# The second attention of a two-layer graph network in a fixed order on three engines, with its routing in seven steps, paced weight loads and later index copies

## The chip, the cores and the metric

The kernel runs on one core of a Trainium2 chip. A core has five engines, each with its own queue of instructions that it takes in order: TensorE (PE in the profile; its weight loads are shown apart as PEld), VectorE (DVE), ScalarE (ACT), GpSimd (POOL), and SyncE (SP), which here only starts DMAs. An engine waits for another, or for a DMA, at a semaphore. The metric is the device time of one execution in microseconds (us); the median of several runs counts.

## The reference

The input is x (2708 rows of 256) and a sparse 0/1 matrix adj (2708 x 2708). All arithmetic is in float32. Two layers, each an attention over the graph and then a mixture of eight experts:

```
x = x + elu(softmax(where(adj > 0, q k^T / 16, -9e15)) v)         # q, k, v from layernorm(x)
x = x + top2_experts_0(layernorm(x))                               # hidden 1024, own layernorm, weights sum to 1
h = layernorm(x) @ W_fc + b_fc
s = (h @ w_att[:256])[:, None] + (h @ w_att[256:])[None, :] + b_att
x = x + softmax(where(adj > 0, s, -1e9), axis=1) @ h               # "the second attention"
x = x + top2_experts_1(layernorm(x))                               # hidden 512, weights = softmax probabilities
```

In the second attention the score of row i and key j is a term of i plus a term of j. The term of i falls out of the softmax, so the numerator is a product of the 0/1 mask with rows `exp(s_j) * h_j`, and the denominator the same product with `exp(s_j)`.

## The kernel before

**Tiles.** The 2708 rows are 22 tiles (NT) of 128, the last of 20. The stages follow one another: first attention, first experts, second attention, second experts, final sum.

**Second attention** (`layer1_attention`, L602 on). The query tiles are taken in groups, `GROUPS = [6, 6, 4, 3, 3]`; this text calls them G0 to G4. Each group runs over all 22 key tiles k. `attend` (L700) multiplies, for each query tile of the group, the mask of key tile k with the two halves (`parts`) of that key's value row, one matmul each (L708), into an accumulator in PSUM; the short last key tile comes at the end (L714). The masks lie in SBUF as fp8 (`mTs`, one per block of 512 queries) and ScalarE turns the piece that a key needs into float32 (`key_masks`, L681), two keys ahead; `m` has six buffers.

G0 is special: `keys_and_values` (L739) also makes the keys' values, one tile per turn of its loop. VectorE takes statistics of the row (`norm_begin`, L209 to L211), GpSimd raises the variance to the power -1/2 (L215), VectorE normalises (`norm_end`, L219), TensorE transposes (L225), ScalarE copies, TensorE multiplies with W_fc (L640), ScalarE applies the exponential (L646 to L648), GpSimd copies the result into `parts` (L653) and adds the bias to the kept row (L654), and VectorE computes the rest that the first part has lost (`second_part`, L660). `PAUSE` dummy matmuls (L747) stand at the start of G0.

**Routing.** When a group is done, `evict` (L731) copies its accumulators out and puts a generator `finish` for each tile into `line`. `line.step()` (L281), called once per key (in G3 and G4 once per two keys), starts a waiting tile every `line.gap` steps and takes each running tile to its next `yield`. For one tile the steps are: `over_sum`; the new row and its statistics (with the power on GpSimd); in `Experts.route` (L916) the normalised row (L219), two index copies on GpSimd (L940) and the second copy of the row (L944); the gate's logits, top two and `sel` (L961 to L982); the exponential on ScalarE (L984); two small matmuls that count the rows before this one (L987, L988), then at once on VectorE the weights, the target rows `to` (L989 to L1002), and two indirect scatters by GpSimd (L1005) into the DRAM buffer `disp`. Row buffers come in six pairs. The tiles of one group are so routed during the next ones.

**Second experts.** Rows are gathered by expert in chunks of 128, called slots. Each slot reads its rows from `disp` (`xg`, by SP, L1168) and its expert's weights (1154 KB) into one of four ring buffers (`ring`, by an indirect DMA of GpSimd, L1153; a slot whose expert is in the buffer already skips the transfer). `open` (L1126), called at the start of G2, makes the ring and guesses the first four experts; `fill` (L1145) loads these by plain DMAs on SP. `begin` (L1118) is called when 14 tiles are routed and a few keys have passed; it runs `place` (L1020), a row of small VectorE operations on the counts that makes the tables `token_row` and `weight_row` for the first 20 slots, and fetches the first three slots' rows and weights. A second call of `place` inside the slots makes the tables of the rest.

**Order.** SP runs in program order throughout. The second experts' slots run in program order on TensorE, ScalarE and VectorE. In the second attention only G0 is in program order (on these three and GpSimd); in G1 to G4 a scheduler orders each engine's instructions by its own estimates. Several of the lines named here are those of helpers.

Of the kernel before, what the change touches and what calls it, by code (L numbers as in the profile page):

```python
# [20 lines left out]
P = 128  # L21
N = 2708
D = 256
# [29 lines left out]
PAUSE = 12  # L53
# [16 lines left out]
def adj_ffn_kernel(ctx: ExitStack, tc: tile.TileContext, a: dict, out: bass.AP):  # L70
# [147 lines left out]
    def normed(dst, src, mean, factor):  # L218
        nc.vector.tensor_scalar(dst, src, mean, factor, op0=ALU.subtract, op1=ALU.mult)  # L219
# [80 lines left out]
    def layer0_attention(line):  # L300
        with ExitStack() as scope, ExitStack() as until_last:
# [237 lines left out]
            for b, (b0, nb, ts_) in enumerate(BLOCKS):  # L539
# [6 lines left out]
                for k in range(NT):  # L546
# [38 lines left out]
                    if b == last and k == LAG + 2:  # L585
                        experts0.open()
                        experts0.begin()
# [14 lines left out]
    def layer1_attention(mTs, kept, line, first_masks):  # L602
        with ExitStack() as scope:
# [32 lines left out]
            def values(t, xT):  # L636
                r = P
                ps = misc.tile([P, GROUP, P], F32, name="misc").rearrange("p g n -> p (g n)")
                for c in range(DC):
                    nc.tensor.matmul(  # L640
                        ps[:r, : VALUES + 1 + E], xT[:, c, :r], wfc[:, c, :],
                        start=(c == 0), stop=(c == DC - 1),
                    )
                e = e_tail if t == NT - 1 else pool.tile([P, VALUES + 1], F32, name="e", bufs=3)
                q, weight = ROWS[t], e[:r, VALUES : VALUES + 1]
                nc.scalar.activation(weight, ps[:r, VALUES : VALUES + 1], AF.Exp)  # L646
                nc.scalar.activation(e[:r, :VALUES], ps[:r, :VALUES], AF.Copy, scale=weight)
                nc.scalar.activation(  # L648
                    logits[:q, t], ps[:q, VALUES + 1 : VALUES + 1 + E], AF.Copy,
                    scale=spread_of[:q, t : t + 1],  # L650
                )
                if t < NT - 1:
                    nc.gpsimd.tensor_copy(parts[:r, t, 0, : VALUES + 1], e[:r])  # L653
                nc.gpsimd.tensor_add(kept[:q, t], kept[:q, t], bfc_b[:q])  # L654
                return e

# [8 lines left out]
            tails = {}  # L665
# [8 lines left out]
            def key_masks(ts_, k):  # L674

                masks = {}
                for b in sorted({t // GROUP for t in ts_}):
# [3 lines left out]
                    nc.scalar.copy(m[:, : q1 - q0], mTs[b][:, k, q0 - b * BN : q1 - b * BN])  # L681
                    masks.update({t: m[:, t * P - q0 : t * P - q0 + ROWS[t]] for t in here})
# [56 lines left out]
            def keys_and_values(ts_, accs):  # L739
# [5 lines left out]
                idle = misc.tile([P, GROUP, P], F32, name="misc").rearrange("p g n -> p (g n)")  # L745
                for _ in range(PAUSE):
                    nc.tensor.matmul(  # L747
                        idle, ident, wfc.rearrange("p c n -> p (c n)")[:, : GROUP * P],
                        start=True, stop=True,
                    )  # L750
                next(masks_of_keys)
                stats, xn, xT, e = {}, {}, {}, {}
                for i in range(-3, NT + LAG1 - 1):
                    if 0 <= i - 1 < NT - 1:
                        second_part(i - 1, e.pop(i - 1))
                    if i + 3 < NT:
                        stats[i + 3] = norm_begin(i + 3)
                    if 0 <= i + 2 < NT:
                        xn[i + 2] = norm_end(i + 2, *stats.pop(i + 2))
                    if 0 <= i + 1 < NT:  # L760
                        xT[i + 1] = columns(i + 1, xn.pop(i + 1))
                    if 0 <= i < NT:
                        e[i] = values(i, xT[i])
# [7 lines left out]
            g0, total, since = 0, None, 0  # L771
            for g, wide in enumerate(GROUPS):
                if g == 2:
# [6 lines left out]
                    guess = experts1.open([i * (n // RING) * E // (n + GROUP) for i in range(RING)])  # L780
# [5 lines left out]
                if g == 0:  # L786
                    with tc.manual_schedule(engines={
                        mybir.EngineType.PE, mybir.EngineType.Activation,
                        mybir.EngineType.DVE, mybir.EngineType.Pool,
                    }):  # L790
                        keys_and_values(ts_, accs)
                for k in range(NT if g else 0):
# [6 lines left out]
                    if g > 0 and not experts1.begun and experts1.routed >= experts1.early:  # L799
                        since += 1  # L800
                        if since > 2:
                            experts1.begin()
# [8 lines left out]
                g0 += wide  # L811

# [38 lines left out]
    class Experts:  # L851
# [64 lines left out]
        def route(self, t, x, logits=None):  # L916
# [19 lines left out]
            else:  # L936
                xt = rows2[0][:r, :D]
                normed(xt, x[:r], mean, once)
            for j in range(2):
                nc.gpsimd.tensor_copy(  # L940
                    rows2[j].bitcast(I32)[:r, D : D + 1],
                    token[:r, 0 if own_norm else j, t : t + 1],
                )
            (nc.vector if own_norm or self.begun else nc.gpsimd).tensor_copy(  # L944
# [43 lines left out]
            nc.tensor.matmul(ps[:, :E], ones, seen, start=False, stop=True)  # L988
            nc.vector.reciprocal(den[:r, 1:2], den[:r, 0:1])  # L989
# [30 lines left out]
        def place(self, s0, s1):  # L1020
# [8 lines left out]
            if all_chunks:  # L1029
# [3 lines left out]
                self.pads = [partial(self.pad, end, e) for e in range(E)]  # L1033
            tab = one.tile([P, NT, E], F32, name="tab")
# [21 lines left out]
            nc.vector.tensor_sub(change, offset[:, 1:], offset[:, : E - 1])  # L1056
            n = s1 - s0
# [5 lines left out]
            nc.vector.tensor_reduce(self.expert[:, s0:s1], passed, AX.X, ALU.add)  # L1063
            row = one.tile([P, n], F32, name=f"row{s0}")
# [23 lines left out]
            else:  # L1088
# [5 lines left out]
                nc.vector.tensor_sub(self.taken, last, first)  # L1094

# [22 lines left out]
        def begin(self):  # L1118
# [3 lines left out]
            self.place(0, FULL_AFTER[self.early])  # L1122
# [3 lines left out]
        def open(self, likely=None):  # L1126
# [12 lines left out]
            if likely:  # L1139
# [3 lines left out]
                return self.fill(likely)  # L1143

        def fill(self, likely):  # L1145

            for i, e in enumerate(likely):
                nc.sync.dma_start(self.ring[i], self.packed_weights[0][e * P : (e + 1) * P, :])
                yield
# [43 lines left out]
        def slots(self, two, ps_mm, ps_tp, ps_acc, line):  # L1193
# [76 lines left out]
            def slot(s, s1):  # L1270
# [18 lines left out]
                if not placed and (not line.busy() or s + AHEAD == n):  # L1289

                    line.finish()
                    self.place(n, SLOTS)
# [125 lines left out]
```

## Time and profile before

| | |
|---|---|
| median of 3 runs | 1299.15 us (1295.99 to 1305.99) |
| the profiled execution, its time | 1312.22 us |
| its span in the profile | 1310.4 us |
| mean granted TensorE clock | 0.968 |
| busy: TensorE, its weight loads, VectorE, ScalarE, GpSimd | 1209.5, 964.8, 543.6, 438.4, 424.3 us |
| first attention, first experts | 0 to 528.9, to 863.9 us |
| second attention, keys and values with G0 | 872.0 to 947.9 us |
| G1, G2, G3, G4 | to 986.6, 1025.3, 1047.9, 1076.1 us |
| second experts | to about 1280 us |
| final sum | to 1310.4 us |

The stage edges are read from the first matmul of each. A row of the profile names line, engine and operation, what it writes and reads, and its shape. "Idle before" is the time that the engine stood still before an instruction, with what ended the wait; the releaser is inferred from semaphores. The granted clock is the share of full speed at which TensorE was let run. Only waits on the engine that sets a stage's end cost time.

### The profile page before, as it was taken

The page shows a single profiled execution, that of the slowest core. Times are in us where ns is not written, and L with a number is a line of the kernel's source. Part 1 is how long each engine was busy: PE and PEld are TensorE (multiplying, and loading weights), DVE is VectorE, ACT ScalarE, POOL GpSimd, SP SyncE. Part 2 cuts the span into 40 slices and gives each one's busy share as a digit, 9 for nine tenths or more (in the row PEclk, how much of TensorE's full clock was granted, in tenths as well). Part 3 has the DMA queues.
Part 4 walks back from the last instruction along what each step waited for, and adds up shares of the span by engine and source line. Part 5 has one row for each costly group of instructions (what it writes and reads, how often), then busy time and mean ns, then how long its engine had stood idle before and what let it go on. Part 6 is the DMA issues. An engine that isn't in the chain of part 4 may idle for free. (4 is left out here: it accounts for less than half of the span.)

```text
span 1310.4 us, 20893 instructions
## 1 busy us (share of the span) xinstructions
PE 1209.5 (92%) x7098; PEld 964.8 (74%) x7098; DVE 543.6 (41%) x2087; ACT 438.4 (33%) x1282; POOL 424.3 (32%) x553
## 2 busy tenths in 40 slices
PE   7999999999999999999999999989986878999990
PEld 4776666566566665799999999958886767899880
DVE  6613833634626435632121212137764656322114
ACT  3222222112112222532323232326653446544440
POOL 4100111110110203443333433335453556555450
PEclk9999999999999999999999999999998988999995
DMA  8601365997937717274668644540004125544457
GB/s 264 222 1 66 106 177 141 247 239 190 247 90 180 152 57 294 79 214 127 214 214 285 191 133 142 166 106 3 2 30 173 38 69 163 178 138 130 136 178 258
DMA packets 107243, 197.83 MB, mean 151 GB/s; under 512 B 26754, under 2 KB 81719, under 8 KB 100987
## 3 DMA queue, kind: packets, MB, share of 16 engines
q1 hardware_dynamic: 77276, 110.09, 30.2%
q0 software_dynamic: 27040, 83.56, 20.1%
q10 hardware_dynamic: 2814, 2.77, 0.7%
q8 instruction: 59, 0.97, 0.3%
q14 instruction: 54, 0.43, 0.1%
HBM read 263.63 MB, written 66.12 MB: 252 GB/s over the span
## 5 line engine op out<-in xcount | busy, mean ns | idle before, releaser
L1224 PEld LDWEIGHTS mm<-xe,ring 128*128 128x128 f32 x2192 | 266.8, 195 | 28.0 <-issue 14.0
L1224 PE MATMUL mm<-xe,ring 128*128 128x128 f32 x2192 | 276.2, 280 | 12.0 <-ACT xe L1211 5.0
L1240 PE MATMUL acc<-ring,hT 128*128 128x256 f32 x1096 | 266.6, 381 | 3.4 <-ACT hT L1232 3.4
L1232 ACT ACTIVATE hT<-mm,ring 128x128 f32<-128x128 f32 x548 | 156.0, 368 | 255.8 <-issue 196.6
L1240 PEld LDWEIGHTS acc<-ring,hT 128*128 128x128 f32 x1096 | 195.1, 191 | 24.1 <-ACT hT L1232 4.0
L447 PE MATMUL s<-g,xnT 128*128 128x512 f32 x420 | 206.4, 606 | 3.3 <-DVE mT L459 3.3
L504 PE MATMUL acc<-v,p 128*128 128x257 f32 (+1 forms) x880 | 209.1, 389 | 0.0
L1246 DVE TENSOR_TENSOR y<-acc,bias 128x256 f32<-128x256 f32 x92 | 39.0, 424 | 361.2 <-PE acc L1240 353.9
L504 PEld LDWEIGHTS acc<-v,p 128*128 128x128 f32 (+1 forms) x880 | 153.3, 190 | 18.1 <-issue 0.8
L1153 POOL DMA_INDIRECT ring<-L_ffn_packed,weight_row x98 | 103.5, 1057 | 186.4 <-issue 150.1
L708 PE MATMUL acc<-parts,m 128*128 128x266 f32 x924 | 134.6, 301 | 15.4 <-ACT m L681 10.4
L708 PEld LDWEIGHTS acc<-parts,m 128*128 128x128 f32 x924 | 121.9, 192 | 23.6 <-ACT m L681 12.3
L215 POOL TENSOR_TENSOR ln_rs<-ln_rs,minus_half 128x2 f32<-128x2 f32 x88 | 65.6, 746 | 219.2 <-DVE ln_rs L211 201.5
L1005 POOL DMA_INDIRECT disp<-row,to x88 | 87.4, 993 | 141.7 <-issue 49.2
L459 DVE TENSOR_SCALAR mT<-s 128x512 fp8e4<-128x512 f32 x105 | 71.9, 687 | 128.0 <-ACT p L458 126.1
L458 ACT ACTIVATE p<-s 128x512 f32<-128x512 f32 x105 | 62.2, 594 | 164.7 <-PE s L453 163.4
L447 PEld LDWEIGHTS s<-g,xnT 128*128 128x128 f32 x420 | 75.3, 192 | 50.2 <-issue 41.9
L1258 POOL DMA_INDIRECT xd<-y,xg x45 | 71.1, 1579 | 77.8 <-issue 30.5
L453 PEld LDWEIGHTS <-apart 128*128 128x128 fp8e4 x420 | 32.7, 99 | 61.2 <-issue 61.2
L681 ACT CAST m<-mT 128x512 fp32r<-128x512 fp8e4 (+4 forms) x168 | 70.4, 471 | 16.9 <-PE acc L708 10.2
L334 DVE TENSOR_SCALAR apart<-adj 128x677 fp8e4<-128x677 int32 x80 | 40.7, 512 | 59.0 <-DMA adj<-in_adj_dram 58.6
L1251 POOL DMA_INDIRECT xd<-y,xg x47 | 47.1, 1003 | 21.6 <-PE tp L1201 7.9
(226 smaller groups left out, 1153.9 us busy)
## 6 DMA issues: line engine op xcount, KB each, us to landing
adj<-in_adj_dram SPq DMA_DIRECT2D x84, 338.5 KB
L_ffn_packed<-in_L_ffn_W_dram SPq DMA_DIRECT2D x16, 1024.0 KB
xg<-disp SPq DMA_DIRECT2D x98, 129.0 KB
L_ffn_packed<-in_L_ffn_W_dram SPq DMA_DIRECT2D x16, 512.0 KB
neighbours<-mT SPq DMA_DIRECT2D x5, 1408.0 KB
mT<-neighbours SPq DMA_DIRECT2D x5, 1408.0 KB
xin<-in_x_dram SPq DMA_DIRECT2D x42, 128.0 KB
ring<-L_ffn_packed SPq DMA_DIRECT2D x4, 1154.0 KB
```

The lines of the kernel that those rows point to most:

```text
L215: nc.gpsimd.tensor_tensor(rs[:r, 1], rs[:r, 0], minus_half[:r], ALU.pow)
L447: nc.tensor.matmul(ps[:kr, :nb], xnT[:, c, k0 : k0 + kr], g[:, c, :nb], start=(c == 0), stop=False,)
L459: nc.vector.tensor_scalar(mT[:kr, k, :], ps[:kr, :nb], -BIG / 2, None, ALU.is_gt, saturate=False,)
L504: nc.tensor.matmul(accs[j][:r], p[keys, q0 : q0 + r], v[keys, k, :], start=(k == 0), stop=(k == NT - 1),)
L681: nc.scalar.copy(m[:, : q1 - q0], mTs[b][:, k, q0 - b * BN : q1 - b * BN])
L708: nc.tensor.matmul(acc[:r], masks[t], parts[:, k, i], start=(k == 0 and i == 0), stop=False,)
L1005: nc.gpsimd.indirect_dma_start(disp[:], bass.IndirectOffsetOnAxis(ap=to[:r, j : j + 1], axis=0), rows2[j][:r], None,)
L1153: nc.gpsimd.indirect_dma_start(w, None, packed[:], bass.IndirectOffsetOnAxis(ap=self.weight_row[:, s : s + 1], axis=0), bounds_check=E * P ...
L1224: nc.tensor.matmul(ps[:, i, :], w[:, c * hidden + f * P : c * hidden + (f + 1) * P], xe[:, c, :], start=(c == 0), stop=(c == DC - 1),)
L1232: nc.scalar.activation(hT[:, f, :], ps[:, i, :], AF.Gelu, bias=w[:, b1 + f : b1 + f + 1])
L1240: nc.tensor.matmul(ps, hT[:, f, :], w[:, w2 + f * D : w2 + (f + 1) * D], start=(f == 0), stop=(f == hc - 1),)
L1258: start = nc.gpsimd.indirect_dma_start(xd[:], at, y, None, bounds_check=N - 1, oob_is_err=False, compute_op=ALU.add)
```

## The change

1. From G0 on, the whole second attention stands in program order on TensorE, ScalarE and VectorE; GpSimd is in program order in G0 alone, as before.
2. `route` yields once more, between the two counting matmuls and the VectorE operations behind them: seven steps instead of six.
3. `place` yields four times. `begin` returns a generator that is stepped once per key in G3 and G4, from the moment that 14 tiles are routed. In the first experts and at the second call it is run through at once.
4. `fill` puts a one-column ScalarE copy ahead of each ring load. It reads the mask that was converted last and writes the ring buffer, so the load waits for it.
5. In layer 1 the index copies depend on the normalised row, so that they stand behind it.
6. In G0 the statistics of a later tile come ahead of `second_part`, and the bias add is a call of its own, one turn later.
7. The dummy matmuls have half the width (256 columns) and write G0's first accumulator; there are 28 at the start, and three more among the first transposes.

```diff
-PAUSE = 12
+PAUSE = 28
...
-                nc.gpsimd.tensor_add(kept[:q, t], kept[:q, t], bfc_b[:q])
                 return e
+
+            def add_bias(t):
+                r = ROWS[t]
+                nc.gpsimd.tensor_add(kept[:r, t], kept[:r, t], bfc_b[:r])
...
                     nc.scalar.copy(m[:, : q1 - q0], mTs[b][:, k, q0 - b * BN : q1 - b * BN])
+                    converted_last[0] = m
...
-                idle = misc.tile([P, GROUP, P], F32, name="misc").rearrange("p g n -> p (g n)")
-                for _ in range(PAUSE):
-                    nc.tensor.matmul(
-                        idle, ident, wfc.rearrange("p c n -> p (c n)")[:, : GROUP * P],
-                        start=True, stop=True,
-                    )
+                def busy(n):
+                    for _ in range(n):
+                        nc.tensor.matmul(
+                            accs[0][:, :D], ident, wfc[:, 0, :D], start=True, stop=True
+                        )
+
+                busy(PAUSE)
...
                 for i in range(-3, NT + LAG1 - 1):
+                    if i + 3 < NT:
+                        stats[i + 3] = norm_begin(i + 3)
+                    if 0 <= i - 1 < NT:
+                        add_bias(i - 1)
                     if 0 <= i - 1 < NT - 1:
                         second_part(i - 1, e.pop(i - 1))
-                    if i + 3 < NT:
-                        stats[i + 3] = norm_begin(i + 3)
...
                     if 0 <= i + 1 < NT:
                         xT[i + 1] = columns(i + 1, xn.pop(i + 1))
+                        if i < 1:
+                            busy(1 - i)
...
-            g0, total, since = 0, None, 0
+            scope.enter_context(tc.manual_schedule(engines={
+                mybir.EngineType.PE, mybir.EngineType.Activation, mybir.EngineType.DVE,
+            }))
+            g0, total, beginning = 0, None, None
...
-                    guess = experts1.open([i * (n // RING) * E // (n + GROUP) for i in range(RING)])
+                    guess = experts1.open(
+                        [i * (n // RING) * E // (n + GROUP) for i in range(RING)],
+                        lambda: converted_last[0],
+                    )
...
-                        since += 1
-                        if since > 2:
-                            experts1.begin()
+                        beginning = experts1.begin()
+                    if beginning:
+                        next(beginning, None)
...
+                row = normed(xt, x[:r], mean, once)
             for j in range(2):
-                nc.gpsimd.tensor_copy(
+                index = nc.gpsimd.tensor_copy(
                     rows2[j].bitcast(I32)[:r, D : D + 1],
                     token[:r, 0 if own_norm else j, t : t + 1],
                 )
+                if not own_norm:
+                    tc.add_manual_dep(
+                        index.ins, row.ins.name,
...
+                        reason="no sooner than the row",
+                    )
...
             nc.tensor.matmul(ps[:, :E], ones, seen, start=False, stop=True)
+            if not own_norm:
+                yield
...
-            self.place(0, FULL_AFTER[self.early])
+            return self.begin_steps()
+
+        def begin_steps(self):
+            yield from self.place(0, FULL_AFTER[self.early])
             rows_ = [self.fetch_rows(s) for s in range(AHEAD)]
             self.fetched = [(self.fetch_weights(s), rows_[s]) for s in range(AHEAD)]
...
-        def fill(self, likely):
+        def fill(self, likely, pace):
             for i, e in enumerate(likely):
+                nc.scalar.copy(self.ring[i][:, :1], pace()[:, :1])
                 nc.sync.dma_start(self.ring[i], self.packed_weights[0][e * P : (e + 1) * P, :])
                 yield
```

The four new yields of `place` stand behind the counts (with the ends of the regions), behind the chunk offsets, behind the slots' experts, behind `token_row` (with `taken`), and so ahead of `weight_row`.

## The prediction

> **What bounds the kernel.** I read the busy times by stage first, with stage edges set at the first matmul of each stage in the timeline. Columns: stretch; busy us and instructions of each engine; granted TensorE clock; DMA share; GB/s.
>
> ```profile
> core 0: us, PE busy (x) PEld busy (x) DVE busy (x) ACT busy (x) POOL busy (x), PEclk, DMA share, GB/s
> 528.90:863.90 335.00, 332.89 (x2280) 306.25 (x2280) 87.00 (x329) 114.22 (x380) 128.02 (x105) 0.99 0.57 171
> 872.00:947.90 75.90, 68.96 (x407) 57.61 (x406) 54.35 (x163) 48.45 (x146) 40.29 (x74) 0.93 0.12 38
> 947.90:986.60 38.70, 34.57 (x278) 32.89 (x277) 23.50 (x145) 21.65 (x59) 16.59 (x29) 1.00 0.17 58
> 986.60:1025.30 38.70, 24.89 (x184) 23.41 (x184) 20.75 (x131) 11.13 (x33) 17.19 (x35) 0.87 0.30 121
> 1025.30:1047.90 22.60, 19.30 (x142) 17.70 (x138) 13.69 (x87) 10.41 (x31) 13.21 (x21) 0.92 0.12 42
> 1047.90:1076.10 28.20, 21.43 (x145) 16.58 (x142) 16.90 (x104) 11.63 (x48) 15.11 (x21) 0.89 0.25 72
> 1076.10:1142.20 66.10, 56.06 (x343) 50.01 (x344) 30.52 (x143) 38.62 (x100) 38.65 (x44) 0.89 0.54 167
> ```
>
> TensorE is full in the first experts (332.89 of 335.00) and not in the second attention (keys and values from 872.0; groups G1 to G4 from 947.9, 986.6, 1025.3, 1047.9). G2 has two thirds of G1's matmuls and takes the same 38.7 us. So I asked who TensorE waited for between 947.9 and 1076.1 (total us, times, longest):
>
> ```profile
> PE misc L987 <- DVE sel L982: 11.2, 1, 11.2
> PE acc L708 <- ACT m L681: 10.4, 7, 2.0
> PE acc L708 <- issue: 3.3, 2, 1.7
> ```
>
> Then the timeline around the 11.2 us (start, us, engine, line; in brackets the idle time before it and its releaser):
>
> ```profile
> 989.09 0.41 POOL L940 COPY row<-token 128x1 int32<-128x1 int32 x1 [7.01 <-DMA disp<-row,to]
> 997.17 0.18 POOL L940 COPY row<-token 128x1 int32<-128x1 int32 x1 [5.07 <-DMA disp<-row,to]
> 1001.87 0.72 POOL L215 TENSOR_TENSOR ln_rs<-ln_rs,minus_half 128x2 f32<-128x2 f32 x1
> 1002.63 0.41 DVE L219 TENSOR_SCALAR row<-kept,ln_mv,ln_rs 128x256 f32<-128x256 f32 x1 [12.38 <-POOL ln_rs L215]
> 1004.56 0.17 PE L987 MATMUL misc<-sel,before 128*128 128x8 bf16 x1 [11.23 <-DVE sel L982]
> ```
>
> The chain: an index copy (L940) for a later tile stands in GpSimd's queue ahead of the power of this tile (L215), and waits 7.01 and 5.07 us until an earlier scatter has freed its row buffer. VectorE waits for the power, TensorE for VectorE's `sel`. The scatters are late because the four ring loads (1154 KB each) leave together: DMA share 0.99 to 1.02, 383 to 429 GB/s from 984 to 994. Elsewhere the same copy waits about 1.5 us. The 10.4 us on L681 is ScalarE's order: at 966.72 it waited 3.02 us for VectorE's `p` (L984), with four mask copies behind it, and TensorE waited 1.72 us for them.
>
> **The clock.** The same columns, two falls and what came after:
>
> ```profile
> 875.10:878.50 3.40, 0.85 (x4) 0.40 (x4) 3.15 (x14) 0.91 (x4) 2.20 (x3) 1.00 0.77 230
> 882.00:885.40 3.40, 3.08 (x7) 1.74 (x8) 2.40 (x7) 1.21 (x5) 2.10 (x5) 0.50 0.64 193
> 885.40:888.80 3.40, 3.40 (x12) 2.92 (x13) 2.67 (x8) 1.60 (x6) 2.11 (x4) 0.50 0.00 0
> 1021.90:1025.30 3.40, 1.99 (x18) 1.46 (x18) 2.69 (x20) 1.49 (x7) 1.22 (x3) 1.00 0.00 0
> 1025.30:1028.70 3.40, 3.20 (x16) 2.86 (x13) 3.25 (x19) 3.26 (x10) 2.02 (x2) 0.50 0.22 78
> ```
>
> The clock fell to 0.50 after 3.4 us that held 1.99 us of matmuls, and did not rise after 3.4 us that held 3.08. The Trainium skill ("TensorE: Matmul & The Clock Gate", what's actually happening) says half rate follows a window of about 3.4 us that is idle, full rate one that is busy. By that rule the partial bubble at 1021.9 costs no clock; by the row it costs half of 3.4 us. I take the row: every stall of over about 1.4 us is counted with some clock behind it. Where they differ: a new 3.5 us wait (below) would by the rule hardly cost clock (first expert slots gain 4.5), by the row it does (2.5).
>
> **Part by part, against the profiled execution (1312.22 us).**
>
> *Start of keys and values.* Before: nine dummy matmuls (L747, 0.85 us each) run ahead of TensorE's branch, three behind it; the first real transpose starts at 876.64, matmuls run at half clock from 878.5 to 888.8, and the first attend (L708) starts at 886.72. After: 28 dummies of half the width (0.43 us) all stand behind the branch, three more among the first transposes. TensorE finishes real work at 863.94; its branch took 865.4 to 868.8, so I start the dummies at 869. Half clock until the first full busy window ends (875.1) gives 7.1 of them, the other 20.9 take 8.9: done at 884.0. To the first attend, by program order: transposes, three dummies and two value products 3.8 us, then a bubble, since tile 3's normalised row now stands behind tile 0's `second_part`, which waits for the whole value chain; 6.6 us together: 890.6, 3.9 late. Steady part: from 900 on the period is 3.03 us where TensorE needs 2.63; the 0.2 us waits on `xn` (14 times) come from a loop: statistics, power (0.74) on GpSimd, parts copy (0.40) behind it, `second_part` (0.95), next statistics. With statistics ahead of `second_part`, and the bias add (0.72) moved, that loop opens; VectorE needs 2.4 to 2.55 us a tile. Attend 18: 890.6 + 18 x 2.63 = 937.9 against 940.3: **-2.4**. Bounds: +1 (start at 871.8, one window later) to -6 (clock up a window sooner, no bubble). The middle, since both edges have one near row each.
>
> *G1.* 252 matmuls x 0.1286 = 32.4, tail 1.2, six routing pairs 0.6, eviction 0.4: 34.6 against 38.7. Routing in seven steps puts `sel` two steps ahead of its matmul and the exponential one step ahead of the masks that it could hold up. Per tile VectorE's round (back part 0.8, next tile's `lg` to `sel` 0.85, over_sum 0.7, statistics 1.35, power and its latency 1.0, row 0.4) is 5.1 us beside TensorE's 4.7: it slips 0.4 a tile, 2.2 in six tiles, within a slack of 2.5. **-4.0** (-2 to -4.1).
>
> *G2.* 168 x 0.1286 = 21.6, tail 0.7, rest 1.3: 23.6 against 38.7: **-15.1**; that is 11.2, smaller waits of 2.5, and the half clock from 1004.6 to 1008.2 (1.8). The ring loads now each wait for a one-column ScalarE copy that reads a converted mask, four keys apart: 4.6 us for 1154 KB, which takes 2.8 at 410 GB/s. Nearest row for that copy is a 128x128 mask copy, 0.30: four cost 1.2 us of a ScalarE that is busy 11 of 38.7. The index copies now stand behind the row, so GpSimd's power no longer waits for a landing. The scatter itself has no such cover, nor needs it: its next user is six tiles on. A rule against the pacing: "DMA: Bandwidth & Descriptors" (queues, rings) has each DMA engine take turns between rings by packets. If turns were even, a scatter would land in about 3 us instead of 1.5, and pacing would buy nothing. The row says 7.0 and 5.1; I take it. Bounds -11 (only the long wait goes) to -15.6.
>
> *G3.* 16.2 + 0.7 + 0.8 = 17.7 against 22.6: **-4.9** (waits 1.73, 1.36, 0.2; half clock 1.7). Bounds -3 to -5.
>
> *G4.* Matmuls as in G3, 17.3, but here the early tables come in, some 24 VectorE operations (4 us from 1057 to 1061), now spread over five keys. GpSimd's order has the three ring fetches (1.33 each with their gaps) and tile 14's two scatters (2.6) ahead of tile 16's power: from 10.2 us into the group (`weight_row`) to 16.8, so power at 17.5, `sel` at 20, where TensorE wants it at 16.5. A new wait of 3.5 at L987; behind it stand the tail products and all expert slots. The first chunk (`xg`) is not late: `token_row` at 9.0, loads about 4.5 later by the rows at 1061 to 1065, wanted at 20. 17.3 + 0.4 + 3.5 + 0.5 = 21.7 against 28.2: **-6.5** (-3 to -10). Of the old waits here, 5.1 us are ScalarE's on a releaser that the profile calls remote; nothing in the change touches those by name, so I take 4 off: **-2.5**.
>
> *First expert slots.* 9 us of matmuls ran at half clock after that stall, 4.5 lost; with a 3.5 us wait in front, **-2.5** (0 to -4.5). The exponential/Gelu table switches stay. The second table comes one slot later (3.7 us); its rows are wanted at slot 17, nine slots on: nothing. From 1142 to the end (steady 3.73 us a slot, two DMA stalls) nothing changes but the start.
>
> Sum: 2.4 + 4.0 + 15.1 + 4.9 + 2.5 + 2.5 = **31.4**. Profiled execution about 1281. The median of the runs is 1299.15, 13 us below the profiled one, and I don't know in which waits; the same 31.4 gives **1267.7**.
>
> **Rivals.**
> *A, ScalarE and VectorE still hold up TensorE:* fixed order doesn't remove the 10.4 us on L681, as the exponential stays in line ahead of masks; only ring and index pay: 11.2 + 1.8 + 2.4: about 1283.7. For: VectorE's round (5.1) is longer than TensorE's share (4.7). Against: the extra step's slack.
> *B, all of it:* no remote waits, tile 16 not late, clock full in the slots: 31.4 + 4 + 3.5 + 2 + 2 = 43: about 1256.
> *C, slower:* one mechanism: in fixed order VectorE stands at L219 until GpSimd's power, which stands behind two scatters (2.4) that themselves wait for `to`, which now waits for the scatter of four tiles before to land. With both in the round it is 5.1 + 2.4 and whatever of the landing shows; from 6.55 us a tile on (17 tiles x 1.85 = 31.4) the gain is gone; at 7.5 (no landing at all), 17 x 2.8 = 47.6: 1299 + 16 = about 1315. Against: VectorE's own front part (0.85 + 0.7 + 1.35) runs beside the scatters, and four tiles are over 18 us.
> *D, pacing doesn't pace:* ScalarE may convert up to six masks ahead, so loads could follow at 2.5 us, under their 2.8. Then the queues stay full for 11 us, but the power is no longer behind a landing; VectorE might meet late buffers once: 6 us lost: 1274.
>
> **Numbers.** Forecast 0.60, A 0.17, B 0.10, C 0.05, D 0.08. Range 1253 to 1287: it takes in A and most of B, and leaves out C and a worse start. A measurement of this kernel tells about 1% (13 us) from no change. Faster by over 1% (below 1286): 0.60 + 0.10 + 0.08 + 0.14 of A = 0.92; within 1%: 0.03 of A and 0.02 of C; slower 0.03.
>
> **What would show it.** Right: no idle time over 2 us on L987 in G2, G2 under 25 us; ring loads apart, DMA share well under 1 over 10 us; L225 no longer waiting on `xn`, period 2.63; dummies done near 884, clock 0.50 until about 875. A wait of about 3.5 us at the last L987 of G4. Wrong: L681 waits of 1.5 us or more remain (A); L219 waits for GpSimd of over 3 us in every tile (C); first attend later than 892.

## The result and the profile after

The changed kernel takes **1292.06 us** (median of 9 runs, 1288.55 to 1296.54); beside it the kernel before took 1298.27 (9 runs, 1294.61 to 1305.99). The ratio is 0.9946, with a 95% interval from 0.9922 to 0.9969: 6 us off, within the 1% that the forecast called no change. Forecast were 31.4 us off and 1267.7. Measured again on two chips, each time with the kernel before beside it, the change gave 0.9934 (0.9912 to 0.9955) and 0.9892 (0.9852 to 0.9933). On the last of these chips, called the slower one below, the kernel before took 1312.15 us instead of about 1300, so only ratios and traces are compared between chips.

The profiled execution took 1296.54 us, with a span of 1294.8. The stretches that answer to those of before, edges again at the first matmul of each stage (keys and values with G0, G1, G2, G3, G4 with the hand-over, first expert slots):

```profile
core 0: us, PE busy (x) PEld busy (x) DVE busy (x) ACT busy (x) POOL busy (x), PEclk, DMA share, GB/s
872.00:943.70 71.70, 70.47 (x453) 63.77 (x452) 49.62 (x156) 47.26 (x143) 41.20 (x67) 1.00 0.13 40
943.70:980.10 36.40, 34.08 (x279) 32.88 (x277) 28.71 (x151) 20.96 (x57) 18.21 (x34) 1.00 0.09 33
980.10:1007.60 27.50, 22.52 (x185) 21.74 (x185) 17.52 (x96) 13.01 (x36) 14.12 (x29) 1.00 0.61 218
1007.60:1027.80 20.20, 19.01 (x141) 18.02 (x138) 15.06 (x79) 10.40 (x32) 10.79 (x19) 0.92 0.10 35
1027.80:1059.60 31.80, 20.03 (x144) 16.93 (x142) 24.63 (x133) 11.59 (x50) 19.02 (x30) 0.89 0.21 63
1059.60:1124.40 64.80, 54.37 (x343) 48.24 (x344) 33.70 (x159) 38.91 (x101) 38.49 (x48) 0.92 0.52 170
```

G2 is 11 us shorter, G1 and G3 by 2.3 and 2.4; G4 with the hand-over is 3.6 us longer. VectorE is busy there for 24.63 us where it was busy for 16.90. TensorE's waits from 943.7 to 1062 (total us, times, longest):

```profile
PE misc L1012 <- DVE sel L1007: 12.2, 10, 3.5
PE tp L1237 <- issue: 3.4, 1, 3.4
PE misc L1053 <- DVE seen L1023: 2.9, 1, 2.9
PE acc L713 <- ACT m L685: 0.5, 2, 0.3
```

L1012 is L987 of before, L713 is L708, L685 is L681, L1053 is L1026, L1237 is L1201. The one wait of 11.2 us is gone and so are those on ScalarE's masks (10.4 to 0.5). In their place stand ten smaller waits on VectorE's `sel`, 12.2 us in all, and at the end of G4 a wait of 3.4 that the profile puts down to "issue". TensorE's first transpose of the experts (L1237) needs a PSUM buffer that VectorE's eviction (L739) has to free, and VectorE ends that copy at 1059.5, just before the transpose at 1059.61. (The releaser is inferred here from those times; in a later run, below, the profile itself names the eviction.)

In G2 there is a round. VectorE, GpSimd (start us, us, engine, line; idle time before and its releaser in brackets):

```profile
983.95 0.41 DVE L219 TENSOR_SCALAR row<-kept,ln_mv,ln_rs 128x256 f32<-128x256 f32 x1 [1.04 <-POOL ln_rs L215]
987.00 0.17 DVE L1029 TENSOR_REDUCE to<-hot 128x2 int32<-128x16 f32 x1
987.95 1.04 POOL L1032 DMA_INDIRECT disp<-row,to  x1 [2.88 <-issue]
989.29 0.98 POOL L1032 DMA_INDIRECT disp<-row,to  x1 [0.30 <-issue]
990.29 0.74 POOL L215 TENSOR_TENSOR ln_rs<-ln_rs,minus_half 128x2 f32<-128x2 f32 x1
991.07 0.41 DVE L219 TENSOR_SCALAR row<-kept,ln_mv,ln_rs 128x256 f32<-128x256 f32 x1 [2.56 <-POOL ln_rs L215]
```

From one row (L219) VectorE takes 3.2 us to `to`; 0.8 us later GpSimd starts two scatters, 2.3 us; behind them stands the next tile's power, 0.74; and VectorE waits for it. The round is 991.07 - 983.95 = 7.12 us a tile. TensorE has 5.2 us of matmuls in such a round (5.23 from 998.18 to 1005.28) and waits for the rest: 1.22, 1.88 and 1.88 us on `sel` in three rounds. This is the mechanism of rival C, at a milder size, and no landing is in it.

In G4 VectorE is the bound. The stretches up to the last tail product (1056.2) and on to the first expert product (1060.9), VectorE's waits from 1027.8 to 1060, and TensorE's waits in G4:

```profile
1027.80:1056.20 28.40, 20.03 (x144) 16.91 (x141) 22.02 (x119) 11.59 (x50) 16.35 (x26) 0.94 0.21 63
1056.20:1060.90 4.70, 0.69 (x3) 0.33 (x3) 3.79 (x24) 0.46 (x2) 3.77 (x6) 0.51 0.21 75
...
DVE row L219 <- POOL ln_rs L215: 5.9, 4, 3.5
...
1030.80 0.17 PE L1012 MATMUL misc<-sel,before 128*128 128x8 bf16 x1 [0.51 <-DVE sel L1007]
1035.65 0.17 PE L1053 MATMUL misc<-seen,ones 128*128 128x8 bf16 x1 [2.91 <-DVE seen L1023]
1046.28 0.17 PE L1012 MATMUL misc<-sel,before 128*128 128x8 bf16 x1 [1.30 <-DVE sel L1007]
1054.80 0.17 PE L1012 MATMUL misc<-sel,before 128*128 128x8 bf16 x1 [3.52 <-DVE sel L1007]
```

VectorE is busy for 22.0 us and waits 5.9 (of which 0.8 falls behind 1056.2) for its own power: nearly all of the 28.4. TensorE's side gives the same sum: 20.0 us busy and 8.2 waiting, all of it for VectorE. L1053 is the matmul that counts the rows for the tables; it stands in TensorE's fixed order and needs VectorE's `seen`.

For the experiments below the stages are cut where the traces are sharpest: at the end of the last product of the first experts, the first attend (L713), the end of each group's tail products, the first product of the second experts, and the last matmul. Times in us:

| kernel | to first attend | G0 | G1 | G2 | G3 | G4 | hand-over | to the end | sum |
|---|---|---|---|---|---|---|---|---|---|
| before, first profile | 22.8 | 60.4 | 39.3 | 39.0 | 22.6 | 27.5 | 1.8 | 201.5 | 414.9 |
| before, second profile | 22.4 | 60.1 | 39.2 | 39.0 | 22.3 | 20.9 | 1.6 | 198.8 | 404.3 |
| after | 23.0 | 54.4 | 36.8 | 27.8 | 20.3 | 28.3 | 4.7 | 202.6 | 397.9 |

What lies ahead, the same code in all, ended between 858.2 and 866.2 us; so single spans are not compared below.

### The profile page after: what moved, and what is told of

It is laid out like the page before. It is cut to its first block, busy times and chain, and to the rows that moved or that the text cites. A ratio compares the mean times of both kernels' runs of the same rounds, so it can differ in the third digit from the quotient of the medians.

```text
span 1294.8 us, 20983 instructions
## 1 busy us (share of the span) xinstructions
PE 1204.9 (93%) x7136; PEld 972.2 (75%) x7136; DVE 552.4 (43%) x2087; ACT 439.1 (34%) x1286; POOL 424.3 (33%) x553
## 5 line engine op out<-in xcount | busy, mean ns | idle before, releaser
L1260 PE MATMUL mm<-xe,ring 128*128 128x128 f32 x2192 | 277.7, 281 | 12.2 <-ACT xe L1247 8.7
L1276 PEld LDWEIGHTS acc<-ring,hT 128*128 128x128 f32 x1096 | 195.3, 191 | 23.2 <-ACT hT L1268 3.6
L713 PE MATMUL acc<-parts,m 128*128 128x266 f32 x924 | 129.2, 297 | 1.8 <-DVE raw L739 1.1
L713 PEld LDWEIGHTS acc<-parts,m 128*128 128x128 f32 x924 | 119.5, 190 | 9.2 <-issue 3.3
L685 ACT CAST m<-mT 128x512 fp32r<-128x512 fp8e4 (+4 forms) x168 | 70.6, 473 | 14.1 <-PE acc L713 11.8
```

The source lines that it names most:

```text
L713: nc.tensor.matmul(acc[:r], masks[t], parts[:, k, i], start=(k == 0 and i == 0), stop=False,)
L1260: nc.tensor.matmul(ps[:, i, :], w[:, c * hidden + f * P : c * hidden + (f + 1) * P], xe[:, c, :], start=(c == 0), stop=(c == DC - 1),)
L1276: nc.tensor.matmul(ps, hT[:, f, :], w[:, w2 + f * D : w2 + (f + 1) * D], start=(f == 0), stop=(f == hc - 1),)
```

## The experiments

### Before, profiled again

No edit.

> The kernel before, unchanged, profiled a second time. The first profiled execution took 1312.2 us, 13 above the median of the timed runs (1298.3), while the changed kernel's took 1296.5, 4.5 above its median. Theory S (a draw): the 11.2 us wait in G2 and its half clock are one execution's luck; here the span is nearer 1300, and the idle time of TensorE in G1 to G4 is lower by about as much as the span. Rival F (a fixed surplus): the span is again within 3 us of 1310.4, and the same waits stand in G2 at the same size; then every kernel's profiled run has its own surplus and spans may not be compared with medians.

Measured: 1302.46 us, span 1300.8. Neither theory holds as written. The wait in G2 is there again:

```profile
PE misc L987 <- DVE sel L982: 10.9, 1, 10.9
```

What is gone is 6.6 us in G4 (27.5 to 20.9) and 2.7 in the second experts. In the first profile ScalarE had stood still in G4 for a releaser that the profile shows only as "remote", outside this core; the second profile has no such line. This is the first one's:

```profile
ACT m L681 <- remote: 5.1, 4, 1.9
```

Such lines of over 1 us were seen otherwise only in the traces of the slower chip, up to 8 us long. So some 10 of the 13 us between the first profile and the median (414.9 - 404.3) were one execution's, and no gain could be read from them.

### The power ahead of the scatters

```
 to = tensor_reduce(...)
+if not own_norm:
+    yield
+    yield
 for j in range(2):
     scatter = nc.gpsimd.indirect_dma_start(disp, to[j], row[j])
+    # behind the next tile's power, on the same engine
+    tc.add_manual_dep(scatter.ins, powers[-1].ins.name, ...)
```

> The kernel after, with each tile's two scatters issued two steps later and behind the next tile's power, so that the power no longer stands behind them. Theory L (the loop row L219 -> to -> two scatters -> power -> row L219, 7.1 us a tile in G2): the round falls to 5.5 to 5.9 in G2, G2 takes 24 us instead of 27.5, the waits of 3.5 us (tile 16's count) and 3.4 us (first expert chunk, standing behind VectorE's eviction) in G4 fall under 1.5 each; together 6 to 11 us off, timed about 1284. Rival V (VectorE's own round of 5.6 us with the power's round trip is the limit, the scatters only fill its gap): the round in G2 stays over 6.5 or the gain is under 3 us, timed 1289 to 1293.

Measured: 1283.6 us, ratio 0.9879 (0.984 to 0.9917). The rows in G2:

```profile
986.50 0.41 DVE L221 TENSOR_SCALAR row<-kept,ln_mv,ln_rs 128x256 f32<-128x256 f32 x1 [0.81 <-POOL ln_rs L217]
992.21 0.42 DVE L221 TENSOR_SCALAR row<-kept,ln_mv,ln_rs 128x256 f32<-128x256 f32 x1 [0.84 <-POOL ln_rs L217]
```

The round is 5.7 us; G2 24.5 (after 27.8), G3 19.0 (20.3). The loop is shown for G2. In G4 the expectation failed: 27.8, with a hand-over of 5.2 and a wait of 3.1 on `sel`, although tile 16's power now stood ahead of ring fetches and scatters. VectorE's waits for its power are down to 2.9 us there, but it is busy for 23.4 of the 27.8: its own work sets G4, not the queue of GpSimd.

### Eight steps, newest tile first

```
 def step(self):
-    self.running = [s for s in self.running if next(s, self) is not self]
+    todo = self.running[::-1]               # in the second attention
+    todo = [s for s in todo if next(s, self) is not self]
+    self.running = todo[::-1]
...
 if not own_norm:
     yield
+    yield
 nc.vector.reciprocal(den...)
```

> The kernel after, with one more step between a tile's count and its tail (eight in all), and with the newest tile's step first in each turn, so that the next tile's statistics and power run ahead of this tile's tail and scatters; the power's round trip then lies behind VectorE's tail of 0.85 us. Theory L: VectorE's round falls from 5.6 to about 4.7 in G1, G3 and G4 and from 7.1 to 5.6 in G2; nothing waits over 1 us on the count in G1 to G3: G1 35, G2 24, G3 18.5, G4 25; timed 1280 to 1284. Rival V: as TensorE needs 5.7 a tile in G3 and 5.9 in G2, only the loop with the scatters cost anything, and this is no faster than the run with the power first (within 2 us).

Measured: 1282.62 us, ratio 0.9864 (0.9826 to 0.9902). G1 35.4, G2 25.6, G3 19.3, G4 26.4, hand-over 3.2. By the median it lies a microsecond from the run above, inside both intervals, so that by the time rival V holds as well. G1 is shorter as expected (VectorE's round is 4.6 to 5.0 us there instead of 5.6), G4 is not.

### Pacing and index alone

```
 # before, with two parts of the change
 for i, e in enumerate(likely):
+    nc.scalar.copy(self.ring[i][:, :1], pace()[:, :1])
     nc.sync.dma_start(self.ring[i], ...)
...
+    tc.add_manual_dep(index.ins, row.ins.name, ..., reason="no sooner than the row")
```

> The kernel before with two parts of the change alone: each ring load behind a one-column copy of a converted mask, and the index copies behind the row; order, steps and tables as before. Forecast's term: the long wait of 11.2 us in G2 and its half clock of 1.8 go, 1298.3 - 13 = 1285. Theory S (most of that wait was one profiled execution's): timed 1292 to 1297, and the fixed order and steps account for the rest. Rival: the scheduler moves other things with it and the time rises over 1300.

> The kernel before with the paced ring loads and the index behind the row alone, a second time. Theory G (the fixed order of G1 to G4 with its tables pays in the start, G1 and G3, and loses as much in G4): within 3 us of the changed kernel in this call, by traces 0.2 us apart from the end of the first experts to the first product of the second. Rival W (the whole change is worth its parts): the changed kernel is faster by over 6 us.

Measured: 1287.12 us, 0.9898 (0.9864 to 0.9932), and on another chip 1288.68, 0.9907 (0.9879 to 0.9936), where the whole change took 1291.73. The forecast's term of 13 us is right, and two parts of the change give at least as much as all seven. From the last product of the first experts to the first of the second: 195.1 and 195.7 us, against 195.3 and 196.6 for the whole change. G4 took 19.3 and 22.9.

### Pacing alone, index alone

The first added line above without the second, and the second without the first.

> The kernel before with the paced ring loads alone. If the wait of 11 us in G2 came from the four loads that fill the queues at once, so that a scatter lands late (the forecast's reading of the share of 1.01 at 986 to 992 us), the wait goes with the pacing alone: G2 28 us instead of 39, ratio 0.990 as with both. If the index copies ahead of the row are needed too, a wait of over 4 us on the count stays in G2, ratio 0.993 to 0.999.

Measured: 1297.55 us, 0.9979 (0.9961 to 0.9997). The long wait is halved, not gone; GpSimd's waits for a landing between 980 and 1030, and TensorE's in G2:

```profile
POOL row L944 <- DMA disp<-row,to: 15.0, 5, 6.0
PE misc L991 <- DVE sel L986: 6.3, 1, 6.3
```

> The kernel before with the index copies behind the row alone, the four ring loads still issued at once. If the power stood behind an index copy that waited for a scatter to land, and nothing else waits for that landing, the long wait in G2 goes with this alone: G2 28 to 30 us, ratio 0.990. If the landing is what counts, the row itself or the scatters wait for it instead, VectorE at the row L219, and a wait of 4 to 11 us stays in G2: ratio 0.995 to 1.001.

Measured: 1287.6 us, 0.9904 (0.9875 to 0.9932), as with both. The queues were as full as in before (10 us at a share of 1.01), the scatters landed late (the last number is the median us from issue to landing, of those that have a landing on record), and nobody waited for them; the third line is TensorE's longest wait of G2:

```profile
984.00:994.00 10.00, 9.53 (x81) 8.75 (x80) 8.07 (x44) 5.45 (x14) 5.04 (x10) 1.00 1.01 407
disp<-row,to POOLq DMA_INDIRECT x12, 6.9
PE acc L708 <- ACT m L681: 2.6, 3, 1.9
```

G2 takes 28.5 us. The order of two small copies in GpSimd's queue carried the gain; the pacing adds nothing that can be measured beside it.

### The fixed order, in G4 and everywhere

All of after, but with the order in G4 left to the scheduler; then in all of G1 to G4 (the second edit instead of the first):

```
+if g == 4:
+    fixed.close()          # the manual order ends here
...
-scope.enter_context(tc.manual_schedule(engines={PE, Activation, DVE}))
```

> The kernel after, unchanged, beside the three that follow. Theory G (a fixed order on VectorE costs in the last group, G4, what it gains in G1 and G3): G4 again takes 27 to 29 us from the tails of G3 to its own, and 4 to 5 us more pass before the first expert's products; the kernel before, profiled a second time, took 20.9 and 1.6 there. Rival D (a draw, as the stall in G4 of the first profile of before was): G4 takes 20 to 24 here. Timed about 1292 by both.

> The kernel after, with the fixed order on TensorE, ScalarE and VectorE given up for G4 alone, where the scheduler orders again. Theory G: G4 takes 20 to 22 us and 1.8 us pass to the first expert's products: 9 to 11 us less than after, timed 1281 to 1284. Rival P (it is GpSimd's three ring fetches ahead of tile 16's power, which the scheduler leaves where they are): the wait of 3.5 us stays and the gain is under 5 us, timed over 1286.

Measured on the slower chip: after 1298.56 us, 0.9892, with 29.3 us in G4 and 3.7 in the hand-over, so the long G4 was no draw; with G4 free 1299.96, 0.9895 (0.9869 to 0.9921). By the time this is inconclusive: G4 fell by 2.5 and the hand-over by 2.1 us, and no wait on `sel` is left in G4, against rival P, but ScalarE had waits on a "remote" releaser, of up to 2.6 us in G4 and 4.3 in the experts, and these took 217 us instead of 205.

> The kernel after, unchanged, on the same chip as the three that follow, since two chips have given it ratios of 0.9946 and 0.9892 to the kernel before. In its profile VectorE is busy or waiting for its power for 27.9 of the 28.4 us of G4, so that G4 is again 28 to 29 us and the hand-over to the second experts 4 to 5. Ratio 0.989 to 0.995.

> The kernel after without the fixed order in G1 to G4 (keys and values keep theirs): seven steps, spread tables, pacing, index and start as in after. Theory G: G4 falls to 19 to 21 us and the hand-over to 1.6, G1 and G3 rise to 40 and 22: 3 to 7 us less than after in this call. Rival W: the order carries the gain of G1 to G3, and the time rises by 5 us or more.

Measured on a chip without such lines: after 1291.73 us, 0.9934 (0.9912 to 0.9955), again with 29.3 us in G4 and 3.7 in the hand-over; without the fixed order 1285.23, 0.9887 (0.986 to 0.9913). Theory G holds, except that G3 stayed at 20.0. G1 rises to 40.7 from 36.9 as the old waits on masks come back, G4 falls to 20.8 and the hand-over to 2.2. G4's row (VectorE's is the third pair of busy time and instructions):

```profile
1026.90:1047.70 20.80, 18.08 (x141) 15.26 (x141) 13.55 (x88) 11.70 (x48) 13.56 (x18) 1.00 0.28 84
```

13.55 us in 88 instructions instead of 22.02 in 119. The tables lie in the group in both; but the scheduler has the normalised row of three tiles in it (L219 at 1027.84, 1034.96 and 1039.76) and the next one behind it, at 1054.19, where the fixed order has four in it. TensorE's wait at the tables' count is 0.2 us here instead of 2.9.

### The order alone

```
 # before
+scope.enter_context(tc.manual_schedule(engines={PE, Activation, DVE}))
 g0, total, since = 0, None, 0
```

> The kernel before with the fixed order in G1 to G4 alone (six steps, tables in one go, loads at once, index ahead of the row, start as before). Theory G: G1 falls to 37 us or less, G2 keeps a wait of 8 us or more, G4 rises to 27 or more and the hand-over to 3 to 5; slower than before by 2 to 8 us, ratio 1.002 to 1.006. Rival W: the order pays by itself, ratio 0.995 or less.

Measured: 1296.22 us, 0.9967 (0.9951 to 0.9984): my expectation was on the wrong side. Against the second profile of before G1 fell by 3.7, G2 by 5.7 and G3 by 4.2 us, and 7.2 were lost in G4 and 2.1 in the hand-over; VectorE is busy for 23.5 us of G4's 28.1. The order is worth a little while G2 still has its long wait (7.6 us here instead of 10.9), and costs 6.5 (1291.73 against 1285.23) where the index has already removed that.

### The tables

```
-                        beginning = experts1.begin()
-                    if beginning:
-                        next(beginning, None)
+                        beginning = experts1.begin()
+                        for _ in beginning:
+                            pass
```

> The kernel after, with the early tables and first fetches issued in one go instead of in six steps, all else as after. Theory T (VectorE's 4.3 us of tables are on the path in fixed order, however they are spread): G4 within 2 us of after's 28, timed 1290 to 1294. Rival (spreading pays): TensorE waits 3 to 4 us more at one count in G4, timed 1295 to 1297. Rival (spreading costs, as the fetches come five keys later): the hand-over to the experts is 2 us sooner, timed 1288 to 1290.

Measured: 1296.72 us, 0.9882 (0.9856 to 0.9909), beside 0.9892 for after on the same chip. G4 with the hand-over took 33.9 us instead of 33.0. Six steps or one makes no difference that can be measured.

Now all tables behind G4 (the two lines `if beginning: next(...)` left out, so that the loop behind the group runs them):

> The kernel after with the early tables and first fetches issued behind G4 instead of within it. VectorE is busy for 22.0 and waits for its power for 5.9 of the 28.4 us of G4 in after; the tables are about 4.3 of it, and the three ring fetches no longer stand ahead of tile 16's power (3.5). Theory V (VectorE's own sum sets G4): G4 falls to 20 to 23 us, and the hand-over rises from 4.7 to 10 to 14, as tables, fetch and transfer now follow; time about as after or 3 us longer. Rival Q (something else in the fixed order sets G4, TensorE's own or ScalarE's place): G4 stays over 26.

Measured: 1296.72 us, 0.9956 (0.9928 to 0.9984). G4 fell to 22.2 us, from 28.3 to 29.3 in three profiles of after, and the hand-over rose to 12.8, from 3.7 to 4.7:

```profile
1026.00:1048.70 22.70, 18.88 (x147) 15.76 (x141) 18.26 (x99) 10.93 (x50) 12.73 (x22) 1.00 0.14 47
PE tp L1235 <- DMA xg<-disp: 10.9, 1, 10.9
```

Theory V holds: in the fixed order it is the tables, with the fetches that follow them, that make G4 long. (In the scheduler's order above they lie in a G4 of 20.8 us.) They can't simply be put behind it.

### Both cures together

Both edits from above: eight steps with the newest first, and G4 left to the scheduler (`fixed.close()` at `g == 4`).

> The run with eight steps and the newest tile first (1282.6), with the fixed order given up for G4 as well. If the two causes are separate (the power behind the scatters in G2 and G3, the order in G4), they add: from the end of the first experts to the first product of the second 187.2 - 7 = 180 us, timed 1274 to 1277. If they are one (scatters ahead of the power in G4 too), the time stays at 1281 to 1284.

> Eight steps with the newest tile first, and the fixed order given up in G4, a second time: the first profile had one interruption of 7 to 8 us by a releaser outside the core in the hand-over. Without it 187 - 5 = 182 us from the first experts to the second, 11 to 13 us less than after in this call; if the gain in G4 was not real, it is 6 to 8 less, as the run without this edit would give.

Measured: 1288.9 us, 0.9806 (0.9775 to 0.9837) on the slower chip, with one interruption in the hand-over, in which the profile names the eviction as what TensorE's transpose waits for:

```profile
ACT raw L742 <- remote: 7.3, 1, 7.3
PE tp L1246 <- ACT raw L742: 5.1, 1, 5.1
```

and **1275.97 us, 0.9824** (0.9798 to 0.9851) on the chip where after had 0.9934. It is faster than both kernels. G1 35.4, G2 25.5, G3 19.3, G4 22.6, hand-over 1.6; from first experts to second 181.8 us, as expected. TensorE's three largest waits from 935 to 1045, in place of before's 11.2 and 10.4:

```profile
PE acc L716 <- ACT m L688: 3.1, 2, 2.2
PE acc L716 <- DVE raw L742: 2.2, 3, 1.1
PE mm L1269 <- ACT xe L1256: 1.9, 2, 1.3
```

## Why the prediction was wrong, step by step

By the table's edges the forecast's 31.4 us became 414.9 - 397.9 = 17.0 against the profile that it was made from, and 404.3 - 397.9 = 6.4 against the second profile of before, which is the median's 6. So 25.0 us are missing against the second profile: 9.9 in G4, 9.4 in the hand-over and the slots, 8.4 in G1 to G3, less 2.7 that the start gave more than forecast. The step that failed is the sum for G4 and what follows it; beside it, G2's loop was taken for free, and a gain was carried from one profile to the median.

*Start.* Forecast -2.4; measured 83.2 to 77.4, -5.8. The opened loop gave its 6 us as forecast (period 2.63, no waits on `xn`). From the last of the 28 dummies to the first attend 6.5 us passed, forecast 6.6. What was mis-sized is the time ahead of it. The dummies began 2.4 us after the end of the first experts, not 5.1, and had the half clock for one window, 868.55 to 871.96, not until 875.1. The first attend so came 23.0 us after the first experts, where the forecast had 26.7 and before 22.8.

*G1.* Forecast -4.0; measured -2.5. VectorE's round, summed to 5.1 us, is 5.60 (rows L219 from 953.63 to 976.04, four rounds): its parts were taken half a microsecond too short, against TensorE's 4.7. With the newest tile first the round is 4.6 to 5.0, and G1 gave 35.4 instead of 36.8.

*G2.* Forecast -15.1 (the three parts given for it add up to 15.5); measured -11.2. The 11.2 us wait went, as forecast, and through the index: that link of the chain was right. That the scatters had to land sooner was not: with the index alone they landed as late as ever. Of the 3.9 us missing, 3.3 came back when the power went ahead of the scatters (27.8 to 24.5): they are the loop through the scatters. The prediction dismissed it because "VectorE's own front part (0.85 + 0.7 + 1.35) runs beside the scatters". In G2 nearly all of that front part runs ahead of `to`, so only the new row and its statistics lie beside them.

*G3.* Forecast -4.9; measured -2.3. Of the difference, 1.3 went with the power ahead of the scatters (19.0): TensorE was busy in G3 for 19.1 us at a mean clock of 0.92 in after, and for 17.6 at 1.00 there, without the half clock that G2's last wait left behind.

*G4.* Forecast -2.5; measured +0.8 against the first profile and +7.4 against the second. This is the step that failed. The sum was 17.3 + 0.4 + 3.5 + 0.5 = 21.7 us up to the experts' first transpose. After takes 31.8 to there, with no "remote" wait in it. Of the 10.1 too few, 4.7 are TensorE's waits for VectorE, 8.2 instead of 3.5: the largest that had no term at all is the one at the tables' count, 2.9 us, and it stands in all three profiles of after. Another 3.0 are the wait for the eviction, 3.4 us where the sum has at most 0.4, and about 2 are TensorE busy for longer (20.0), in part at half clock behind these waits. The text named the 24 operations of the tables (4 us) and did not add up VectorE for the whole group: 22.0 us busy and 5.9 waiting. The wait for tile 16 did come, through the chain that was forecast (three ring fetches and two scatters ahead of its power, at 1051.29, some 6 us later in the group than expected). That it came at 3.52 is luck: the longest waits on `sel` in G4 in the other two profiles of after are 1.3 and 2.9. The gain of 4 us from ScalarE's "remote" waits was read from one execution.

*Hand-over and slots.* Forecast -2.5; measured +2.9 and +1.1. The eviction stands behind late routing on VectorE, and a stall next to the experts costs clock as well. Columns as in the first fence. The first two rows lie in G2, the next three at the end of G2 and the start of G3, three more at the end of G4 and in the first slots; the last two are from the slots of the second run with pacing and index alone:

```profile
998.27:1001.68 3.41, 2.02 (x18) 2.02 (x18) 3.17 (x20) 2.32 (x7) 0.63 (x3) 1.00 0.26 101
1001.68:1005.09 3.41, 3.21 (x26) 3.09 (x26) 0.98 (x5) 0.47 (x2) 2.59 (x3) 1.00 0.14 47
1005.09:1008.50 3.41, 1.73 (x17) 1.35 (x17) 2.98 (x20) 1.52 (x6) 0.79 (x4) 1.00 0.09 31
1008.50:1011.91 3.41, 3.41 (x18) 3.41 (x17) 1.95 (x7) 2.09 (x6) 2.31 (x3) 0.50 0.13 44
1011.91:1015.32 3.41, 3.41 (x31) 3.35 (x29) 2.73 (x15) 1.75 (x6) 1.07 (x4) 1.00 0.11 39
1052.90:1056.30 3.40, 1.39 (x8) 0.51 (x7) 3.23 (x22) 0.68 (x3) 2.33 (x5) 1.00 0.09 27
1056.30:1069.90 13.60, 8.63 (x37) 7.86 (x38) 6.00 (x30) 6.52 (x13) 4.80 (x9) 0.50 0.10 34
1069.90:1073.30 3.40, 3.40 (x26) 3.18 (x25) 1.05 (x5) 1.81 (x6) 0.43 (x1) 0.99 0.00 0
...
1087.68:1091.09 3.41, 1.32 (x7) 0.82 (x5) 2.04 (x12) 3.38 (x7) 2.75 (x3) 1.00 0.89 348
1091.09:1094.50 3.41, 3.01 (x24) 2.90 (x25) 1.41 (x10) 1.59 (x5) 2.69 (x5) 1.00 0.50 135
```

The forecast took the row against the rule of the Trainium skill ("TensorE: Matmul & The Clock Gate", what's actually happening), that an idle window halves the rate and a busy one restores it. The row was right to take: windows that held 1.73 and 1.39 us of matmuls, and so were not idle, were followed by half clock, for one window where the next was full, and for 13.6 us where it wasn't. The latter cost about half of 8.63, 4.3 us by estimate, at the head of the experts. But the row is no threshold: after windows that held 2.02 and 1.32 us the clock stayed at 1.00. So "every stall of over about 1.4 us" counts too many; what decides is not shown here.

*From the profile to the median.* The sum was carried over unchanged, with the remark that the 13 us between them lay in unknown waits. The second profile shows them: 6.6 in G4, 2.7 in the experts. A gain in G4 could not be had from a median that never contained its stall.

*The rivals.* A said that ScalarE and VectorE would still hold up TensorE. ScalarE didn't (0.5 us); VectorE did, in ten waits on `sel` (12.2 us) and at the tables' count (2.9). C's mechanism was in place, at 7.1 us a tile in G2 alone; the forecast gave it 0.05 as a whole and should have carried its mild form as a cost. D's premise was right in so far as the loads were not apart (DMA share 0.84, 0.97 and 0.65 in three stretches of 6 us from 980 on; the first two loads were issued 2.3 us apart), and it cost nothing, since nothing stood behind a landing any more.

## What to carry to other kernels

Before a fixed order is put on an engine, add up that engine's own work for each stage, with the waits for what it sends away and needs back, and set the sum beside the bound of the stage: an order that removes waits in one stage can make that engine the bound of the next. In a queue that runs in order, ask what stands ahead of the one short operation on which a loop depends; moving two copies, or two scatters, from ahead of it to behind it gave most of what could be had here. Profile the kernel before twice before reading a gain from a wait whose releaser the profile does not name.

## What was not expected of the hardware

- Beside the ring loads a scatter took 5.2 to 8.7 us from issue to landing, whether the loads were paced or not: 8.7 and 6.9 with the index alone, 6.7 in the second profile of before, 7.1 and 5.9 in after, 7.7 and 5.2 with pacing alone. With no load under way it took about 2.5; the prediction's 1.5 is the wait of a copy, not a landing. (Only some scatters have a landing on record.) It cost nothing once no queue stood behind a landing. The Trainium skill ("DMA: Bandwidth & Descriptors", queues and rings) has each DMA engine take turns between rings by packets; from that the prediction estimated a factor of two, and measured is 2.1 to 3.5.
- The same kernel took 1298.3 to 1300.7 us in four sets of runs and 1312.2 on another chip, about 0.9% more. The change was worth 0.5 to 0.7% in two of the four, where it was timed, and 1.1% on the slower chip; the intervals overlap. Why ScalarE and VectorE stand still there for up to 8 us stays open.
